# A graph-network stack on one Trainium2 core: one score slot in four joined into a single tile

## The chip, the cores and the metric

The kernel runs on one core of one Trainium2 chip. The metric is the device time of one launch in microseconds (us). The engines are TensorE (PE), VectorE (DVE), ScalarE (ACT) and GpSimd (POOL); SyncE (SP) issues most of the DMAs.

## The reference

Input x is 64 graphs of 256 nodes with 128 features, and one 256 x 256 matrix adj is shared by all. Four layers follow each other, each of the form x = x + L(relu(layernorm(x))). Layer 0 is a gated recurrence of five steps, layer 1 a Chebyshev filter, layer 2 a graph convolution with normalised rows. Layer 3 is pairwise attention, and most of the time is spent in it:

```python
s1 = jnp.einsum('bkf,ef->bke', x, W1)        # W = adj, W1, W2 its two halves
s2 = jnp.einsum('bkf,ef->bke', x, W2)
pre = s1[:, :, None, :] + s2[:, None, :, :] + b_lin
h = jnp.where(pre >= 0, pre, ALPHA * pre)     # ALPHA = 0.2
e = jnp.einsum('bije,e->bij', h, a) + bias
attn = jax.nn.softmax(e, axis=2)
out = jax.nn.sigmoid(jnp.einsum('bij,bjf->bif', attn, x))
```

For each graph, a score is needed for each pair (i, j) of 256 nodes; it is a sum over 256 features e of a leaky relu, weighted with a[e].

## The kernel before, in words

Two graphs make a pair; there are 32 pairs. The part of the score that is linear in s1 and s2 goes its own way (the row `lin`). What is left of the leaky relu is max(0, pre) with weight 0.8 a[e], and max(0, s1 + s2) is, up to terms that depend on one index or vanish in the softmax, -min(s1, -s2). So the work is a minimum per (graph, i, j, e), and then a weighted sum over e.

The 256 features are two **halves** of 128, one feature per partition: half 0 uses s1a and s2a, half 1 uses s1b and s2n. A **slot** is four nodes i (32 apart) of both graphs of a pair: for one half that is a tile `rl` of 128 partitions x 2048 numbers (4 nodes, 2 graphs, 256 nodes j). A pair has 64 slots, in two blocks of 32 (`ic`), and the whole kernel 2048 slots, so 4096 half-tiles. Three engines make them (`work_on_tile`, L723):

- VectorE makes half 0 in one instruction (L738), min(s1a, s2a), with s2a read in the PSUM bank that TensorE wrote it to (`s2v`, one bank for each parity of the pair).
- ScalarE makes either half with eight activations of 256 numbers (L751), relu(s1 - s2-type operand). For half 1 it reads `s2p`, a copy in a PSUM bank of its own (L745); for half 0 it reads `s2c`, a copy in SBUF that it makes once in a pair (L590).
- GpSimd makes half 1 with eight instructions of 256 numbers (L758), min(s2n, s1b) from SBUF and then max with the most negative number, which changes nothing.

TensorE sums each tile over the features with four matmuls (`score`, L783; L796) into one of two PSUM banks. Their weights are `win` or `win_n`, zero but for one column, which holds 0.8 a[e] or its negative; the window of 32 columns selects the row that the slot's node gets. After 64 tiles a block is full, and its `tail` (L635) makes the softmax and the output.

For each pair `front` (L392) computes the first three layers and the operands of the fourth; its last steps, from L584, write s2a, s2c, the row `lin`, s2n, s1b and s1a. `front` and `tail` are generators that yield before each step the engine and the time from which it can run.

The order of all instructions is fixed when the program is written. A planner (L846 to L876) keeps a clock for each engine, adds to it the cost written beside each step (`ran`, L101), and always lets the engine whose clock is earliest choose. Tails go ahead of fronts, and fronts ahead of tiles. `half` (L710) says which half an engine takes: VectorE half 0, GpSimd half 1, ScalarE half 1 unless half 0 is two slots or more behind (`LAG`). `MOST` bounds how many unscored tiles an engine may hold, and 13 tiles are shared by all. TensorE scores the tile that is ready earliest by that clock. `in_order` (L128) then binds each engine to the order found; the waits between engines come from who writes and reads which tile.

Of the kernel before, what the change touches and what calls it, by code (L numbers as in the profile page):

```python
# [8 lines left out]
F32 = mybir.dt.float32  # L9
# [8 lines left out]
LN_EPS = 1e-5  # L18
NORM_EPS = 1e-12
ALPHA = 0.2  # L20
LEAST = -3.4028234663852886e38
PE, DVE, ACT, POOL = ENGINES = (mybir.EngineType.PE, mybir.EngineType.DVE, mybir.EngineType.Activation, mybir.EngineType.Pool)
SLOTS = 64


@with_exitstack
def kernel(
# [168 lines left out]
    u5t = const.tile([P, P], F32, name="u5t")  # L196
    gate_b = const.tile([P, 3], F32, name="gate_b")
    bz, br, bh = gate_b[:, 0:1], gate_b[:, 1:2], gate_b[:, 2:3]
    th = const.tile([P, 3, D], F32, name="th")
    win = const.tile([P, NE, 63], F32, name="win")  # L200
    win_n = const.tile([P, NE, 63], F32, name="win_n")
    w2n = const.tile([P, N], F32, name="w2n")
    g2 = const.tile([P, P], F32, name="g2")
    SET_UP = set()

    def first_constants():
# [43 lines left out]
    def other_constants():  # L250

        yield DVE, 0.0, 0, lambda: "first" in SET_UP
        for c in range(NC):
            nc.vector.tensor_copy(adj_ti[:, c, :], adj_t[:, c, :])
            nc.vector.tensor_add(adj_ti[:, c, c * P:(c + 1) * P], adj_t[:, c, c * P:(c + 1) * P], ident)
        t = ran(DVE, 0.8)

        for c in range(NC):
            yield PE, t, 1
            b = take()  # L260
            for k in range(NC):
# [11 lines left out]
        nc.vector.memset(win, 0.0)  # L273
        nc.vector.memset(win_n, 0.0)
        nc.vector.tensor_scalar(w2n, adj_t[:, 1, :], -1.0, None, op0=OP.mult)
        ran(DVE, 0.6)
        yield DVE, clock[DVE]
        a_rep = work.tile([P, NE, P], F32, name="a_rep", tag="short", bufs=12)
        nc.vector.memset(a_rep, 1.0)
        for k in range(NE):  # L280
            nc.vector.tensor_scalar(win[:, k, 31:32], acol[:, k:k + 1], 1.0 - ALPHA, None, op0=OP.mult)
            nc.vector.tensor_scalar(win_n[:, k, 31:32], acol[:, k:k + 1], ALPHA - 1.0, None, op0=OP.mult)
            nc.vector.tensor_scalar(a_rep[:, k, :], a_rep[:, k, :], acol[:, k:k + 1], None, op0=OP.mult)
        t = ran(DVE, 1.2)

        yield PE, t, 1
# [3 lines left out]
        t = ran(PE, 0.8, t, b[1])  # L290
        yield DVE, t
        nc.vector.tensor_scalar(g2, b[0][:, 0:P], ALPHA, None, op0=OP.mult)
        t = ran(DVE, 0.25, t)
        spare.append([b[0], t])
        SET_UP.add("all")
# [51 lines left out]
    def tok(name, **kw):  # L347
        return work.tile([P, NB, NC, D], F32, name=name, **kw)
# [43 lines left out]
    def front(p):  # L392
# [101 lines left out]
                t_h = ran(ACT, COPY, t)  # L494
                spare.append([b[0], t_h])
        yield DVE, t
        x1 = tok("x1")
# [34 lines left out]
        x2 = tok("x2")  # L532
# [55 lines left out]
        yield ACT, t_s2a  # L588
        s2c = feat("s2c")
        nc.scalar.copy(s2c, by_feature(s2a))  # L590
        t_s2c = t_s2a = ran(ACT, COPY, t_s2a)
        yield PE, t_hT, 1
        b = take()
        for g in range(4):
            nc.tensor.matmul(b[0][g * 32:(g + 1) * 32, 0:P], g2[:, 0:32], flat(hT)[:, g * P:(g + 1) * P],  # L595
                             start=True, stop=True, skip_group_check=True)
        t = ran(PE, 0.22, t_hT, b[1])
        yield ACT, t
# [12 lines left out]
        t = ran(PE, PROJECT, t_hT, b[1])  # L611
        yield ACT, t
        s2n, t_2 = copied("s2n", b, t)
        yield PE, t_hT, 1
        b = take()
        project(b[0], adj_t[:, 0, P:2 * P], hT)
        t = ran(PE, PROJECT, t_hT, b[1])
        yield ACT, t
        s1b = feat("s1b")
        nc.scalar.activation(s1b, by_feature(b[0]), AF.Identity, bias=blin[:, 1:2], scale=1.0)  # L620
        t_b = ran(ACT, BIASED, t)
        spare.append([b[0], t_b])
        yield PE, t_hT, 1
        b = take()
        project(b[0], adj_t[:, 0, 0:P], hT)
        t = ran(PE, PROJECT, t_hT, b[1])
        yield ACT, t
        s1a = feat("s1a")
        nc.scalar.activation(s1a, by_feature(b[0]), AF.Identity, bias=blin[:, 0:1], scale=1.0)  # L629
        t_n = ran(ACT, BIASED, t)  # L630
        spare.append([b[0], t_n])
        READY[p] = dict(x3=x3, h3=h3, hT=hT, s1=(s1a, s1b), s2a=by_feature(s2a), s2c=s2c, s2n=s2n, lin=lin, t_lin=t_lin,
                        since=(max(t_n, t_s2a, t_s2c), max(t_b, t_2)))

    def tail(p, ic, pe, since, x3, h3):  # L635

# [56 lines left out]

    NSLOT = NPAIR * SLOTS
    tiles = [[relu_pool.tile([P, 4, NB, N], F32, name=f"rl{k}", bufs=1), 0.0] for k in range(13)]
    MOST = {DVE: 8, ACT: 3, POOL: 2}
    held = dict.fromkeys(MOST, 0)
    following = [0, 0]
    begun = {}
    made = []  # L700
    left = {}
    t_pe = {}
    LAG = 2
    t_s2v = [0.0, 0.0]
    TAILED = set()

    def where(n):
        return n // SLOTS, n % SLOTS // 32, n % 32

    def half(e):  # L710

        return 0 if e == DVE or e == ACT and following[0] <= following[1] - LAG else 1

    def tile_ready(e):

        if e in begun:
            return 0.0
        n = following[half(e)]
        if n >= NSLOT or n // SLOTS not in READY or held[e] == MOST[e] or not tiles:
            return None  # L720
        return max(READY[n // SLOTS]["since"][half(e)], min(t[1] for t in tiles))

    def work_on_tile(e):  # L723
        if e not in begun:
            k = half(e)
            tiles.sort(key=lambda t: t[1])
            begun[e] = [following[k], k, *tiles.pop(0), 0]
            following[k] += 1
# [5 lines left out]
        since = max(ops["since"][k], free)  # L734
        if e == DVE:
            whole = [P, 4, NB, N]
            rows = ops["s1"][0][:, :, i0:i0 + 97:32].rearrange("p b g -> p g b").unsqueeze(3)
            nc.vector.tensor_tensor(t, rows.to_broadcast(whole), ops["s2a"].unsqueeze(1).to_broadcast(whole), op=OP.min)  # L738
            done = ran(DVE, 2.2, since)
            t_s2v[p % 2] = done  # L740
            parts = 1
        elif e == ACT:
            if k and "s2p" not in ops:
                ops["s2p"] = s2p
                nc.scalar.copy(s2p, ops["s2n"])  # L745
                ran(ACT, COPY, since)
            parts = 2
            for g in (2 * part, 2 * part + 1):
                for b in range(NB):
                    i = i0 + g * 32  # L750
                    nc.scalar.activation(t[:, g, b, :], (s2p if k else ops["s2c"])[:, b, :], AF.Relu,  # L751
                                         bias=ops["s1"][k][:, b, i:i + 1], scale=-1.0)
            done = ran(ACT, 1.43 if k else 1.6, since)
        else:
            parts = 4
            for b in range(NB):
                i = i0 + part * 32
                nc.gpsimd.tensor_scalar(t[:, part, b, :], ops["s2n"][:, b, :], ops["s1"][1][:, b, i:i + 1], LEAST,  # L758
                                        op0=OP.min, op1=OP.max)
            done = ran(POOL, 0.9, since)  # L760
        begun[e][4] += 1
        if part + 1 == parts:
            del begun[e]
            made.append((done, n, k, t, e))

    def score_ready():

# [15 lines left out]
    def score(tile_):  # L783
# [5 lines left out]
        if first:  # L789
            left[block] = 64  # L790
        made.remove(tile_)
        left[block] -= 1

        w = win if e == ACT else win_n
        for g in range(4):
            nc.tensor.matmul(pe[g * 32:(g + 1) * 32, :], w[:, k, 31 - r:63 - r], flat(t[:, g]),  # L796
                             start=first, stop=(left[block] == 0), skip_group_check=True)
# [3 lines left out]
        scored[0] += 1  # L801
        if left[block] == 0:
            begin((p, ic), tail(p, ic, pe, free, READY[p]["x3"], READY[p]["h3"]))

# [103 lines left out]
```

## Time and profile before

| | |
|---|---|
| median of three runs | 5241.63 us (5241.58 to 5242.08) |
| profiled execution, its time | 5241.64 us |
| profiled execution, its span | 5239.9 us |
| TensorE clock granted, mean | 0.998 |
| GpSimd waiting for a tile that TensorE frees (L758) | 994.9 us, 384 times |
| GpSimd waiting for ScalarE in the recurrence (L474) | 347.6 us, 93 times |
| ScalarE waiting for a tile that TensorE frees (L751) | 137.9 us, 203 times |
| first tile begun | 120 us after the start |

A group of the profile is read so: line, engine, operation, output <- inputs, shapes, count; then busy time in all and the mean ns of one, and then the idle time of the engine before such instructions and what ended it. Neighbours on one engine overlap a little, so busy time divided by count is less than the mean of one, and is the one that adds up. A matmul of float32 leaves two records; a half-tile is eight of L796.

### The profile page before, as it was taken

What the parts mean: (1) busy time and instruction counts of PE and PEld (TensorE: products, weight loads), DVE (VectorE), ACT (ScalarE), POOL (GpSimd) and SP (SyncE); (2) the same over time, 40 slices, a digit from 0 to 9 for tenths busy, and PEclk for the clock granted to TensorE, in tenths of its full rate; (3) what the DMA queues carried; (4) which work ended last, traced back from release to release, by engine and by line L of the source; (5) the groups of instructions that cost most, each with busy time, mean ns of one, the idle gap of its engine ahead of it and who ended that gap; (6) DMA issues with size and microseconds to landing.
All of it is one profiled execution on the core that took longest, in us unless ns stands there. A gap on an engine that the chain in (4) does not pass through costs nothing.

```text
span 5239.9 us, 138951 instructions
## 1 busy us (share of the span) xinstructions
PE 5197.2 (99%) x56085; PEld 1856.9 (35%) x56085; DVE 5140.0 (98%) x4180; ACT 4563.7 (87%) x11785; POOL 3635.0 (69%) x7606
## 2 busy tenths in 40 slices
PE   7999999999999999999999999999999999999999
PEld 3333333333333333333333333333333333333333
DVE  3999999999999999999999999999999999999999
ACT  4888888888888888888888888888888888889899
POOL 2776766666766767667677676776666767767698
PEclk9999999999999999999999999999999999999999
DMA  0000000000000000000000000000000000000000
GB/s 20 7 8 5 8 8 5 8 5 8 8 5 8 5 8 8 5 8 7 6 8 6 8 8 5 8 8 5 8 5 8 8 5 8 6 7 6 5 6 4
DMA packets 60343, 37.48 MB, mean 7 GB/s; under 512 B 4528, under 2 KB 59696, under 8 KB 59696
## 3 DMA queue, kind: packets, MB, share of 16 engines
q1 hardware_dynamic: 58976, 28.59, 2.3%
q8 instruction: 438, 7.18, 0.6%
q14 instruction: 209, 1.71, 0.1%
q10 hardware_dynamic: 720, 0.00, 0.0%
HBM read 18.09 MB, written 10.49 MB: 5 GB/s over the span
## 4 chain that ended last, share of the span: by engine, by line
PE 92%; ACT 5%; DVE 2%; issue 0%; POOL 0%; DMA 0%; ACTq 0%; POOLq 0%
PE bank L796 61%; PE bank L306 27%; ACT rl L751 5%; PE bank L334 2%; DVE rl L738 2%; PE bank L327 1%; POOL rl L758 0%; PE bank L595 0%; DVE hT L481 0%; DVE stats L366 0%; ACT h L493 0%; DMA xin<-in_x_dram 0%; DVE bank L477 0%; DVE x L569 0%; POOL mv L301 0%
## 5 line engine op out<-in xcount | busy, mean ns | idle before, releaser
L738 DVE TENSOR_TENSOR rl<-s1a,bank 128x2048 f32<-128x2048 f32 x2028 | 4505.3, 2277 | 10.4 <-ACT s1a L629 10.1
L751 ACT ACTIVATE rl<-bank,s1b 128x256 f32<-128x256 f32 x9608 | 3691.7, 605 | 139.0 <-PE bank L796 137.9
L758 POOL TENSOR_SCALAR rl<-s2n,s1b 128x256 f32<-128x256 f32 x6776 | 3057.5, 475 | 1025.1 <-PE bank L796 994.9
L796 PE MATMUL bank<-rl,win_n 128*32 128x512 f32 x23000 | 2764.7, 593 | 6.2 <-DVE rl L738 6.0
L796 PE MATMUL bank<-rl,win 128*32 128x512 f32 x9768 | 1282.5, 593 | 0.0
L796 PEld LDWEIGHTS bank<-rl,win_n 128*32 128x32 f32 x23000 | 735.1, 110 | 1543.1 <-issue 1297.6
L796 PEld LDWEIGHTS bank<-rl,win 128*32 128x32 f32 x9768 | 307.0, 110 | 656.3 <-issue 620.7
L474 POOL TENSOR_TENSOR d<-d,hT 128x512 f32<-128x512 f32 x155 | 199.2, 1285 | 347.6 <-ACT d L470 347.6
L306 PE MATMUL bank<-mT,wts 128*32 128x512 f32 x2560 | 332.4, 592 | 0.0
L306 PE MATMUL bank<-adj_t,h 128*32 128x256 f32 x5120 | 309.5, 383 | 3.1 <-ACT h L493 3.1
L306 PEld LDWEIGHTS bank<-adj_t,h 128*32 128x32 f32 x5120 | 166.3, 111 | 164.2 <-issue 52.5
L383 ACT COPY mT<-bank 128x512 f32<-128x512 f32 x160 | 101.0, 631 | 99.4 <-PE bank L306 59.7
L377 ACT ACTIVATE h<-x,mv 128x128 f32<-128x128 f32 x384 | 172.0, 635 | 5.5 <-POOL mv L373 5.5
L657 ACT ACTIVATE sc<-sc,nmx 128x256 f32<-128x256 f32 x128 | 59.5, 523 | 132.5 <-DVE nmx L653 132.5
L306 PE MATMUL bank<-hT,wts 128*32 128x512 f32 x1280 | 167.1, 593 | 0.0
L306 PE MATMUL bank<-mT,w 128*32 128x512 f32 x1280 | 166.7, 592 | 0.0
L306 PE MATMUL bank<-rh,u5t 128*32 128x512 f32 x1280 | 166.6, 592 | 0.0
L493 ACT COPY h<-bank 128x512 f32<-128x512 f32 x128 | 92.1, 720 | 77.1 <-PE bank L334 76.8
L458 ACT ACTIVATE bank<-bank,gate_b 128x512 f32<-128x512 f32 x160 | 117.6, 735 | 44.2 <-PE bank L306 44.2
L306 PEld LDWEIGHTS bank<-mT,wts 128*32 128x32 f32 x2560 | 82.6, 110 | 192.1 <-issue 150.5
L435 ACT ACTIVATE bank<-bank,gate_b 128x512 f32<-128x512 f32 x160 | 118.8, 742 | 30.0 <-ACT rl L751 20.9
L301 POOL TENSOR_TENSOR mv<-mv,minus_half 128x4 f32<-128x4 f32 x128 | 133.0, 1039 | 10.7
(118 smaller groups left out, 3046.4 us busy)
## 6 DMA issues: line engine op xcount, KB each, us to landing
xin<-in_x_dram SPq DMA_DIRECT2D x64, 128.0 KB, 2.2
lin<-row SPq DMA_DIRECT2D x32, 256.0 KB, 7.7
out_dram<-o SPq DMA_DIRECT2D x64, 128.0 KB, 1.8
row<-quarter SPq DMA_DIRECT2D x32, 64.0 KB, 1.5
w_raw<-in_L_gnn_w_w_dram SPq DMA_DIRECT2D x3, 128.0 KB, 2.8
th_raw<-in_L_gnn_Theta_dram SPq DMA_DIRECT2D x1, 320.0 KB, 3.8
adj_n<-in_adj_dram SPq DMA_DIRECT2D x1, 256.0 KB, 3.4
w_raw<-in_L_gnn_u_w_dram SPq DMA_DIRECT2D x2, 64.0 KB, 3.0
```

Source lines behind the costliest of these rows:

```text
L301: nc.gpsimd.tensor_tensor(t, t, minus_half, op=OP.pow)
L306: nc.tensor.matmul(o[g:g + 32], w[:, g:g + 32], t, start=start, stop=stop, skip_group_check=True)
L334: nc.tensor.transpose(pt[:, b, c, :], ht[:, b, c * P:(c + 1) * P], ident)
L377: nc.scalar.activation(h[:, k, :], s[:, k, :], AF.Relu, bias=mv[:, k, 0:1], scale=mv[:, k, 1:2])
L383: nc.scalar.copy(c, by_feature(bank[0]))
L435: nc.scalar.activation(r[0], pr[0], AF.Tanh, bias=br, scale=0.5)
L458: nc.scalar.activation(pr[0], pr[0], AF.Tanh, bias=bz, scale=0.5)
L474: nc.gpsimd.tensor_sub(d, d, hT)
L738: nc.vector.tensor_tensor(t, rows.to_broadcast(whole), ops["s2a"].unsqueeze(1).to_broadcast(whole), op=OP.min)
L751: nc.scalar.activation(t[:, g, b, :], (s2p if k else ops["s2c"])[:, b, :], AF.Relu, bias=ops["s1"][k][:, b, i:i + 1], scale=-1.0)
L758: nc.gpsimd.tensor_scalar(t[:, part, b, :], ops["s2n"][:, b, :], ops["s1"][1][:, b, i:i + 1], LEAST, op0=OP.min, op1=OP.max)
L796: nc.tensor.matmul(pe[g * 32:(g + 1) * 32, :], w[:, k, 31 - r:63 - r], flat(t[:, g]), start=first, stop=(left[block] == 0), skip_group_che ...
```

## The change

Of every four slots one is **joined**. In a joined slot GpSimd makes half 1 as before, and VectorE then adds its minimum of half 0 into the same tile: eight `scalar_tensor_tensor` of 256 numbers, (s2a min s1a) + tile. TensorE sums this one tile in place of two. The other slots (`ALONE`) are made in two halves as before.

For one sum to serve both halves, the weights of the two halves on one partition may differ in sign only. The size 0.8 |a[e]| is therefore multiplied into the operands: `w1` and `w2n` are built in the set-up from adj_n scaled by `size` and transposed, and the bias becomes `blin_s`. `win` then holds only signs, and `win_n` the negative sign of half 0. Where the two signs on a partition differ (`rho` = -1), GpSimd's half must be negated: it reads `s2z` = rho x s2n, and clamps between two per-partition numbers, `s1h` and `s1l`, computed for each pair on VectorE from s1b with `never`.

Besides: `s2c` is gone, and ScalarE's half 0 reads s2a in the bank `s2v`, as VectorE does; its planned cost is 1.43 for either half. GpSimd may hold 4 tiles (before 2). It takes the next joined slot if that is at most `AHEAD_OF` = 4 slots past the next half 1 that stands alone, else that half 1. VectorE takes a finished partner tile before anything else, under a like condition. x1 and x2 share a tag of three buffers, th lies in th_raw, and win_n and g2 are smaller.

```diff
+SHARE = (1, 4)
+AHEAD_OF = 4
...
-        s2c = feat("s2c")
-        nc.scalar.copy(s2c, by_feature(s2a))
-        t_s2c = t_s2a = ran(ACT, COPY, t_s2a)
...
+        s2z = feat("s2z")
+        nc.gpsimd.tensor_scalar(s2z, s2n, rho, 1.0, op0=OP.mult, op1=OP.mult)
+        t_z = ran(POOL, 0.65, t_2)
...
-        nc.scalar.activation(s1b, by_feature(b[0]), AF.Identity, bias=blin[:, 1:2], scale=1.0)
+        nc.scalar.activation(s1b, by_feature(b[0]), AF.Identity, bias=blin_s[:, 1:2], scale=1.0)
...
+        s1h, s1l = feat("s1h"), feat("s1l")
+        nc.vector.tensor_scalar(s1h, s1b, never, None, op0=OP.max)
+        nc.vector.tensor_scalar(s1l, s1b, -1.0, never, op0=OP.mult, op1=OP.min)
+        t_z = max(t_z, ran(DVE, 0.8, t_b))
...
-    MOST = {DVE: 8, ACT: 3, POOL: 2}
+    MOST = {DVE: 8, ACT: 3, POOL: 4}
...
+    def part_of(e):
+
+        if e == DVE:
+            return 0
+        if e == ACT:
+            return 0 if following[0] <= following[1] - LAG else 1
+        return 2 if slot(2) <= slot(1) + AHEAD_OF else 1
...
-        if e == DVE:
+        if e == DVE and k == 2:
+            since = max(ops["since"][0], free)
+            parts = 2
+            for g in (2 * part, 2 * part + 1):
+                for b in range(NB):
+                    i = i0 + g * 32
+                    nc.vector.scalar_tensor_tensor(t[:, g, b, :], ops["s2a"][:, b, :], ops["s1"][0][:, b, i:i + 1], t[:, g, b, :],
+                                                   op0=OP.min, op1=OP.add)
+            done = ran(DVE, 1.55, since)
...
-                    nc.scalar.activation(t[:, g, b, :], (s2p if k else ops["s2c"])[:, b, :], AF.Relu,
+                    nc.scalar.activation(t[:, g, b, :], (s2p if k else ops["s2a"])[:, b, :], AF.Relu,
                                          bias=ops["s1"][k][:, b, i:i + 1], scale=-1.0)
-            done = ran(ACT, 1.43 if k else 1.6, since)
+            done = ran(ACT, 1.43, since)
...
-                nc.gpsimd.tensor_scalar(t[:, part, b, :], ops["s2n"][:, b, :], ops["s1"][1][:, b, i:i + 1], LEAST,
+                nc.gpsimd.tensor_scalar(t[:, part, b, :], ops["s2z"][:, b, :], ops["s1h"][:, b, i:i + 1], ops["s1l"][:, b, i:i + 1],
                                         op0=OP.min, op1=OP.max)
...
-            made.append((done, n, k, t, e))
+            if e == POOL and k == 2:
+                partners.append((done, n, t))
+            else:
+                made.append((done, n, k, t, e))
...
-        left[block] -= 1
-
-        w = win if e == ACT else win_n
+        left[block] -= 2 if k == 2 else 1
+
+        w = win[:, k] if e == ACT else win_n
```

More of the change, by code (lines that the diff above doesn't have):

```diff
@@ L20 @@
 ALPHA = 0.2
-LEAST = -3.4028234663852886e38
+MOST_NEGATIVE = -3.4028234663852886e38
 PE, DVE, ACT, POOL = ENGINES = (mybir.EngineType.PE, mybir.EngineType.DVE, mybir.EngineType.Activation, mybir.EngineType.Pool)
 SLOTS = 64
+SHARE = (1, 4)
+AHEAD_OF = 4
 @with_exitstack
@@ L198 @@
     bz, br, bh = gate_b[:, 0:1], gate_b[:, 1:2], gate_b[:, 2:3]
-    th = const.tile([P, 3, D], F32, name="th")
+    th = th_raw[:, 0:3, :]
     win = const.tile([P, NE, 63], F32, name="win")
-    win_n = const.tile([P, NE, 63], F32, name="win_n")
+    win_n = const.tile([P, 63], F32, name="win_n")
+    w1 = const.tile([P, N], F32, name="w1")
     w2n = const.tile([P, N], F32, name="w2n")
-    g2 = const.tile([P, P], F32, name="g2")
+    g2 = const.tile([P, 32], F32, name="g2")
+    signs = const.tile([P, NE + 2], F32, name="signs")
+    rho, never = signs[:, NE:NE + 1], signs[:, NE + 1:NE + 2]
+    blin_s = const.tile([P, NE], F32, name="blin_s")
     SET_UP = set()
@@ L272, in other_constants @@
         yield DVE, clock[DVE]
[L273 to L277, printed above, removed]
         a_rep = work.tile([P, NE, P], F32, name="a_rep", tag="short", bufs=12)
@@ L280, in other_constants @@
         for k in range(NE):
-            nc.vector.tensor_scalar(win[:, k, 31:32], acol[:, k:k + 1], 1.0 - ALPHA, None, op0=OP.mult)
-            nc.vector.tensor_scalar(win_n[:, k, 31:32], acol[:, k:k + 1], ALPHA - 1.0, None, op0=OP.mult)
             nc.vector.tensor_scalar(a_rep[:, k, :], a_rep[:, k, :], acol[:, k:k + 1], None, op0=OP.mult)
-        t = ran(DVE, 1.2)
-        yield PE, t, 1
+        t_a = ran(DVE, 0.9)
+        yield DVE, clock[DVE]
+        nc.vector.memset(win, 0.0)
+        nc.vector.memset(win_n, 0.0)
+        nc.vector.tensor_scalar(signs[:, 0:NE], acol, 0.0, None, op0=OP.is_ge)
+        nc.vector.tensor_scalar(signs[:, 0:NE], signs[:, 0:NE], 2.0, -1.0, op0=OP.mult, op1=OP.add)
+        nc.vector.tensor_mul(rho, signs[:, 0:1], signs[:, 1:2])
+        nc.vector.tensor_scalar(never, rho, MOST_NEGATIVE, None, op0=OP.mult)
+        size = work.tile([P, NE], F32, name="size")
+        nc.vector.tensor_mul(size, acol, signs[:, 0:NE])
+        nc.vector.tensor_scalar(size, size, 1.0 - ALPHA, None, op0=OP.mult)
+        nc.vector.tensor_mul(blin_s, blin, size)
+        adj_s = work.tile([P, NE, N], F32, name="adj_s", tag="short", bufs=12)
+        for k in range(NE):
+            nc.vector.tensor_copy(win[:, k, 31:32], signs[:, k:k + 1])
+            nc.vector.tensor_scalar(adj_s[:, k, :], adj_n[:, k, :], size[:, k:k + 1], None, op0=OP.mult)
+        nc.vector.tensor_scalar(win_n[:, 31:32], signs[:, 0:1], -1.0, None, op0=OP.mult)
+        t = ran(DVE, 2.4)
+        for c in range(NC):
+            yield PE, t, 1
+            b = take()
+            for k in range(NE):
+                nc.tensor.transpose(b[0][:, k * P:(k + 1) * P], adj_s[:, k, c * P:(c + 1) * P], ident)
+            t = ran(PE, 0.4, t, b[1])
+            yield DVE, t
+            if c:
+                nc.vector.tensor_scalar(w2n, b[0][:, 0:N], -1.0, None, op0=OP.mult)
+            else:
+                nc.vector.tensor_copy(w1, b[0][:, 0:N])
+            t = ran(DVE, 0.35, t)
+            spare.append([b[0], t])
+        yield PE, t_a, 1
         b = take()
@@ L289, in other_constants @@
             nc.tensor.matmul(b[0][:, 0:P], adj_n[:, k, P:2 * P], a_rep[:, k, :], start=(k == 0), stop=(k == NE - 1))
-        t = ran(PE, 0.8, t, b[1])
+        t = ran(PE, 0.8, t_a, b[1])
         yield DVE, t
-        nc.vector.tensor_scalar(g2, b[0][:, 0:P], ALPHA, None, op0=OP.mult)
+        nc.vector.tensor_scalar(g2, b[0][:, 0:32], ALPHA, None, op0=OP.mult)
         t = ran(DVE, 0.25, t)
@@ L496, in front @@
         yield DVE, t
-        x1 = tok("x1")
+        x1 = tok("x1", tag="x12", bufs=3)
         nc.vector.tensor_add(x1, x0, by_token(b[0]))
@@ L531, in front @@
         yield DVE, clock[DVE]
-        x2 = tok("x2")
+        x2 = tok("x2", tag="x12", bufs=3)
         nc.vector.scalar_tensor_tensor(x2, by_token(po[0]), 0.0, x1, op0=OP.max, op1=OP.add)
@@ L587, in front @@
         t_s2a = ran(PE, PROJECT, t_hT, t_s2v[p % 2])
-        yield ACT, t_s2a
-        s2c = feat("s2c")
-        nc.scalar.copy(s2c, by_feature(s2a))
-        t_s2c = t_s2a = ran(ACT, COPY, t_s2a)
         yield PE, t_hT, 1
@@ L594, in front @@
         for g in range(4):
-            nc.tensor.matmul(b[0][g * 32:(g + 1) * 32, 0:P], g2[:, 0:32], flat(hT)[:, g * P:(g + 1) * P],
+            nc.tensor.matmul(b[0][g * 32:(g + 1) * 32, 0:P], g2, flat(hT)[:, g * P:(g + 1) * P],
                              start=True, stop=True, skip_group_check=True)
@@ L613, in front @@
         s2n, t_2 = copied("s2n", b, t)
+        yield POOL, t_2
+        s2z = feat("s2z")
+        nc.gpsimd.tensor_scalar(s2z, s2n, rho, 1.0, op0=OP.mult, op1=OP.mult)
+        t_z = ran(POOL, 0.65, t_2)
         yield PE, t_hT, 1
         b = take()
-        project(b[0], adj_t[:, 0, P:2 * P], hT)
+        project(b[0], w1[:, P:2 * P], hT)
         t = ran(PE, PROJECT, t_hT, b[1])
@@ L619, in front @@
         s1b = feat("s1b")
-        nc.scalar.activation(s1b, by_feature(b[0]), AF.Identity, bias=blin[:, 1:2], scale=1.0)
+        nc.scalar.activation(s1b, by_feature(b[0]), AF.Identity, bias=blin_s[:, 1:2], scale=1.0)
         t_b = ran(ACT, BIASED, t)
         spare.append([b[0], t_b])
+        yield DVE, t_b
+        s1h, s1l = feat("s1h"), feat("s1l")
+        nc.vector.tensor_scalar(s1h, s1b, never, None, op0=OP.max)
+        nc.vector.tensor_scalar(s1l, s1b, -1.0, never, op0=OP.mult, op1=OP.min)
+        t_z = max(t_z, ran(DVE, 0.8, t_b))
         yield PE, t_hT, 1
         b = take()
-        project(b[0], adj_t[:, 0, 0:P], hT)
+        project(b[0], w1[:, 0:P], hT)
         t = ran(PE, PROJECT, t_hT, b[1])
@@ L628, in front @@
         s1a = feat("s1a")
-        nc.scalar.activation(s1a, by_feature(b[0]), AF.Identity, bias=blin[:, 0:1], scale=1.0)
+        nc.scalar.activation(s1a, by_feature(b[0]), AF.Identity, bias=blin_s[:, 0:1], scale=1.0)
         t_n = ran(ACT, BIASED, t)
         spare.append([b[0], t_n])
-        READY[p] = dict(x3=x3, h3=h3, hT=hT, s1=(s1a, s1b), s2a=by_feature(s2a), s2c=s2c, s2n=s2n, lin=lin, t_lin=t_lin,
-                        since=(max(t_n, t_s2a, t_s2c), max(t_b, t_2)))
+        READY[p] = dict(x3=x3, h3=h3, hT=hT, s1=(s1a, s1b), s2a=by_feature(s2a), s2n=s2n, s2z=s2z, s1h=s1h, s1l=s1l,
+                        lin=lin, t_lin=t_lin, since=(max(t_n, t_s2a), max(t_b, t_2), t_z))
     def tail(p, ic, pe, since, x3, h3):
@@ L695 @@
     tiles = [[relu_pool.tile([P, 4, NB, N], F32, name=f"rl{k}", bufs=1), 0.0] for k in range(13)]
-    MOST = {DVE: 8, ACT: 3, POOL: 2}
+    MOST = {DVE: 8, ACT: 3, POOL: 4}
     held = dict.fromkeys(MOST, 0)
-    following = [0, 0]
     begun = {}
     made = []
+    partners = []
     left = {}
@@ L705, with slot @@
     TAILED = set()
+    ALONE, JOINED = [], []
+    for n in range(NSLOT):
+        (JOINED if (n + 1) * SHARE[0] // SHARE[1] > n * SHARE[0] // SHARE[1] else ALONE).append(n)
+    following = [0, 0, 0]
     def where(n):
         return n // SLOTS, n % SLOTS // 32, n % 32
-    def half(e):
-        return 0 if e == DVE or e == ACT and following[0] <= following[1] - LAG else 1
+    def slot(k):
+        of = JOINED if k == 2 else ALONE
+        return of[following[k]] if following[k] < len(of) else NSLOT
+    def part_of(e):
[4 more added lines that the diff above has]
+        return 2 if slot(2) <= slot(1) + AHEAD_OF else 1
     def tile_ready(e):
@@ L717, in tile_ready @@
             return 0.0
-        n = following[half(e)]
+        if e == DVE and partners and min(partners)[1] <= slot(0) + AHEAD_OF:
+            return min(partners)[0]
+        k = part_of(e)
+        n = slot(k)
         if n >= NSLOT or n // SLOTS not in READY or held[e] == MOST[e] or not tiles:
             return None
-        return max(READY[n // SLOTS]["since"][half(e)], min(t[1] for t in tiles))
+        since = READY[n // SLOTS]["since"]
+        return max(since[2] if e == POOL else since[k], min(t[1] for t in tiles))
     def work_on_tile(e):
         if e not in begun:
[L725 to L728, printed above, removed]
+            if e == DVE and partners and min(partners)[1] <= slot(0) + AHEAD_OF:
+                since, n, t = partners.pop(partners.index(min(partners)))
+                held[POOL] -= 1
+                begun[e] = [n, 2, t, since, 0]
+            else:
+                k = part_of(e)
+                tiles.sort(key=lambda t: t[1])
+                begun[e] = [slot(k), k, *tiles.pop(0), 0]
+                following[k] += 1
             held[e] += 1
@@ L733, in work_on_tile @@
         i0 = ic * P + r
-        since = max(ops["since"][k], free)
-        if e == DVE:
+        if e == DVE and k == 2:
[7 more added lines that the diff above has]
+            done = ran(DVE, 1.55, since)
+            t_s2v[p % 2] = max(t_s2v[p % 2], done)
+        elif e == DVE:
+            since = max(ops["since"][k], free)
             whole = [P, 4, NB, N]
@@ L739, in work_on_tile @@
             done = ran(DVE, 2.2, since)
-            t_s2v[p % 2] = done
+            t_s2v[p % 2] = max(t_s2v[p % 2], done)
             parts = 1
         elif e == ACT:
+            since = max(ops["since"][k], free)
             if k and "s2p" not in ops:
@@ L750, in work_on_tile @@
                     i = i0 + g * 32
-                    nc.scalar.activation(t[:, g, b, :], (s2p if k else ops["s2c"])[:, b, :], AF.Relu,
+                    nc.scalar.activation(t[:, g, b, :], (s2p if k else ops["s2a"])[:, b, :], AF.Relu,
                                          bias=ops["s1"][k][:, b, i:i + 1], scale=-1.0)
-            done = ran(ACT, 1.43 if k else 1.6, since)
+            done = ran(ACT, 1.43, since)
+            if k == 0:
+                t_s2v[p % 2] = max(t_s2v[p % 2], done)
         else:
+            since = max(ops["since"][2], free)
             parts = 4
@@ L763, in work_on_tile @@
             del begun[e]
-            made.append((done, n, k, t, e))
+            if e == POOL and k == 2:
+                partners.append((done, n, t))
+            else:
+                made.append((done, n, k, t, e))
     def score_ready():
@@ L791, in score @@
         made.remove(tile_)
-        left[block] -= 1
-        w = win if e == ACT else win_n
+        left[block] -= 2 if k == 2 else 1
+        w = win[:, k] if e == ACT else win_n
         for g in range(4):
-            nc.tensor.matmul(pe[g * 32:(g + 1) * 32, :], w[:, k, 31 - r:63 - r], flat(t[:, g]),
+            nc.tensor.matmul(pe[g * 32:(g + 1) * 32, :], w[:, 31 - r:63 - r], flat(t[:, g]),
                              start=first, stop=(left[block] == 0), skip_group_check=True)
@@ L800, in score @@
         held[e] -= 1
-        scored[0] += 1
+        scored[0] += 2 if k == 2 else 1
         if left[block] == 0:
```

## The prediction

> **What bounds the kernel now.** I read the page first: the busy shares, then the chain that ended last.
>
> ```profile
> PE 5197.2 (99%) x56085; PEld 1856.9 (35%) x56085; DVE 5140.0 (98%) x4180; ACT 4563.7 (87%) x11785; POOL 3635.0 (69%) x7606
> ...
> PE 92%; ACT 5%; DVE 2%; issue 0%; POOL 0%; DMA 0%; ACTq 0%; POOLq 0%
> ```
>
> The chain is 92% PE, so TensorE sets the end; VectorE is as full, but the chain hardly visits it. The table of windows shows the same balance in the middle:
>
> ```profile
> 2000.00:3000.00 1000.00, 999.16 (x10803) 355.78 (x10796) 998.56 (x797) 877.44 (x2270) 693.63 (x1447) 1.00 0.03 7
> ```
>
> Then the groups by form, which price the tiles:
>
> ```profile
> L738 DVE TENSOR_TENSOR rl<-s1a,bank 128x2048 f32<-128x2048 f32 x2028 | 4505.3, 2277 | 10.4 <-ACT s1a L629 10.1 <-issue 0.3
> L751 ACT ACTIVATE rl<-bank,s1b 128x256 f32<-128x256 f32 x9608 | 3691.7, 605 | 139.0 <-PE bank L796 137.9
> L758 POOL TENSOR_SCALAR rl<-s2n,s1b 128x256 f32<-128x256 f32 x6776 | 3057.5, 475 | 1025.1 <-PE bank L796 994.9 <-ACT s1b L620 8.3 <-ACT rl L751 6.5
> ...
> L751 ACT ACTIVATE rl<-s2c,s1a 128x256 f32<-128x256 f32 x160 | 79.9, 1146 | 0.0
> ```
>
> There are 2048 slots of two half-tiles. VectorE makes 2028 first halves at 4505.3/2028 = 2.22 us each (busy time over count: neighbours overlap, so the mean of one is longer). ScalarE makes 9608/8 = 1201 second halves at 3.07 us and 160/8 = 20 first halves; GpSimd 847 at 3.61 us, with 995 us of waiting for a tile that PE frees. The last row matters most: ScalarE's first halves come from s2c, a copy in SBUF, and nearly none exist. VectorE reads the same numbers in the PSUM bank itself. So today no bank is read by both.
>
> PE's price comes from the chain in order of time, VectorE's from its timeline:
>
> ```profile
> 2513.68 10.30 PE bank L796 x96
> ```
> ```profile
> 2510.34 0.68 DVE L439 SCALAR_TENSOR_TENSOR rh<-bank,hT 128x512 f32<-128x512 f32 x1
> 2510.94 11.07 DVE L738 TENSOR_TENSOR rl<-s1a,bank 128x2048 f32<-128x2048 f32 x5
> ```
> ```profile
> 5033.00 1.12 DVE L569 SCALAR_TENSOR_TENSOR x<-bank,rn,x 128x128 f32<-128x128 f32 x4
> 5034.03 2.28 DVE L738 TENSOR_TENSOR rl<-s1a,bank 128x2048 f32<-128x2048 f32 x1
> ```
>
> 96 records are 12 tiles of 8, so 0.858 us a tile. L439 occupies VectorE from start to next start for 0.60 us at 512 elements, L569 (with a per-partition scalar) 1.03/4 = 0.258 us at 128.
>
> **What the Trainium skill says.** "PSUM — Partial Sum Buffer", section "PSUM bank collisions raise a hardware error": two engines on one bank and 32-partition quadrant at once collide, ScalarE reads against VectorE reads included, without arbitration; the compiler back end therefore adds a dependency between any two such instructions, "reads and writes alike". The trace of before can't confirm it: the only rows that could share the bank read s2c instead. "VectorE: DVE Perf Modes", section "The perf-mode tier table": a tensor_tensor with a PSUM operand runs at 1x. It agrees: 2048 elements in 2.20 us. "GPSIMD Engine Reference", section "Key points": GpSimd contends with VectorE instructions that have two SBUF inputs. L738 has one SBUF and one PSUM input, and L758 stays at 463 to 506 ns; the new instruction has the same pair, so I add nothing.
>
> **The change, part by part.** The sum is made against the profiled execution: 5241.64 us, span 5239.9, equal to the median 5241.63.
>
> *PE.* 512 of 2048 slots are joined: 512 tiles fewer at 0.858 us = -439 us. All of it lies on the path. The two set-up transposes lie in the first 120 us, where PE waits anyway; at most 2 us. PE's floor: 5241.6 - 439 = 4802 us.
>
> *VectorE.* A joined half costs 8 scalar_tensor_tensor of 256 elements with a per-partition scalar. L738's slope is 2.20 us/2048 = 1.07 ns per element. L569 at 128 elements is 0.137 of that plus a fixed 0.12; so at 256 elements 0.27 + 0.12 = 0.39 us, and 3.13 us for the eight. Bounds: 0.33 (with the fixed part of L439, 0.60 - 512 x 0.00107 = 0.05, which has no such scalar) and 0.48 (with the whole record of L569, 0.343, as if nothing overlapped); 512 x 8 x 0.09 = 370 us at the upper one. 512 x 3.13 = 1603 us. s1h and s1l add 64 instructions of 512 elements at up to 0.60 (L439's) = 38 us. Other work is 5140.0 - 4505.3 = 635. Idle at start and end is 95 (80 + 12, rounded up). The some fifteen small set-up operations hide in the start; 3 us if they don't.
>
> *ScalarE.* s2c's 32 copies go (25 us). First halves are now read from VectorE's bank. How many? The planner gives ScalarE a first half when VectorE is two behind. If its plan comes to about 4850 us (the PE floor and 1%), VectorE has room for (4850 - 95 - 673 - 1603)/2.22 = 1116 of the 1536 alone, and ScalarE takes n = 420.
>
> *GpSimd.* 512 x 3.61 us for the joined halves go first, the rest for second halves. Its second pointer scalar: between 0 and the 0.06 us that L569 shows over L439; taken as 0, since GpSimd has 31% free. s2z is 32 instructions below 0.95 us (twice L758), 30 us at most, hidden in the front's slack.
>
> *The new waits.* VectorE waits for GpSimd's half; the planner queues it only when its clock says done, and that clock (3.6 us) is L758's. Behind it all of VectorE's queue would stand, and PE behind that; I count 0, at most 0.5 us x 512 = 256 if the second scalar costs its bound. The other wait isn't in the planner's clock: **if reads of one bank exclude each other, every batch of four ScalarE activations on a first half must stand between two VectorE instructions.** Behind VectorE's head stand its tiles, the partners and the front's steps, thus everybody. The length of a batch:
>
> ```profile
> 2554.12 0.91 ACT L657 ACTIVATE sc<-sc,nmx 128x256 f32<-128x256 f32 x2 [1.80 <-DVE nmx L653]
> 2554.94 1.54 ACT L751 ACTIVATE rl<-bank,s1b 128x256 f32<-128x256 f32 x4
> ```
>
> A batch lasts 1.54 to 1.58 us. Handover to ScalarE: L653 ended at 2554.09, L657 began at 2554.12, 0.03; back, L470's end to L474's start on GpSimd is 0.07. VectorE also loses the 0.08 by which the record of L738 overhangs its 2.20. One gap is 0.03 + 1.56 + 0.07 + 0.08 = 1.74 us; two batches in a row 3.2. With a 1.43 us batch in the plan, VectorE's next 2.2 us instruction comes between the two in 0.65 of cases, so a tile costs VectorE 0.65 x 3.48 + 0.35 x 3.2 = 3.38 us. Some is filled with its steps that don't touch the bank (673 of 4850 us, 14%): I take 10% off, leaving 3.05. Bounds: 0 to all 673 us hidden.
>
> Sum on VectorE, n = 420: 95 + 673 + 1603 + 1116 x 2.2215 + 420 x 3.05 = 2371 + 2479 + 1281 = **6131 us**. As a function of n it is 5783 + 0.83n: a first half handed to ScalarE costs VectorE more than making it. So n matters little (300: 6032; 500: 6198). I say 6130; own range 5600 (nearly all other VectorE work inside the gaps) to 6600 (further stalls because a fixed order with two-way waits also passes on ScalarE's delays).
>
> The rest costs nothing on this path: x1 and x2 share three buffers (the third reuse waits for the x2 of the pair before, on VectorE itself, long done); th lies in th_raw; win_n and g2 shrink; w1, blin_s are set up once; no DMA is added or moved, SP's queue keeps its order.
>
> **Rivals.** *A, reads exclude each other*, 6130 us. For: the skill's page, and the diff, which takes away the copy and with it the only separation of the two readers. Against: the planner's clock has no such wait, and no trace here shows one.
>
> *B, the reads run side by side.* Then supply decides. With VectorE (T - 2371)/2.22, ScalarE (T - 95 - 767)/3.05, GpSimd (T - 95 - 608 - 1848)/3.61 equal to 3072 halves together, T = 4860 if all three never wait; with 2% of idle 4950. This is **faster**, by 5.5%. It decides if ScalarE's batches begin while VectorE reads the bank. For: PE loses 439 us for certain, and ScalarE and GpSimd have 13% and 31% idle. Against: the three idle shares vanish together.
>
> *C, exclusion, but mostly beside other work.* The bank itself is taken 1603 + 2479 + 420 x 2.86 = 5283 us, with the first 120 us about 5400. For: 673 us of VectorE and most of ScalarE don't need the bank. Against: the order is fixed, so overlap needs luck.
>
> *The change doesn't do what it says*: joined slots could be few if GpSimd lagged. The list of slots is fixed in the text at 512, so this has no weight.
>
> **How the numbers follow.** A 0.78, B 0.14, C 0.07, and 0.01 that gains and waits cancel. About 0.2% is what a measurement of this kernel can tell from no change. Faster 0.14, same 0.01, slower 0.85. The range takes C and A with their bounds, 5250 to 6600, and leaves out B and a little of A's upper tail.
>
> **What would show it.** Right: VectorE idle of over 1000 us before rl, released by ScalarE's activations, and ScalarE idle before first halves, released by VectorE; some 3300 activations on bank and s1a; PE near 78% busy; the chain divided between DVE and ACT; the new instruction near 0.39 us. Wrong: those activations beside VectorE's instructions on the same bank without a wait (then B), or few of them at all (then about 5800 or less).

## The result, and the profile after

The changed kernel takes 6100.69 us in the median of four runs (6098.29 to 6101.25), the kernel before 5241.85 beside it: 1.164 times as long, with a 95% interval of 1.162 to 1.166. The forecast was 6130 us. The profiled execution has a span of 6099.1 us.

First the busy shares and the chain on the page of the changed kernel, to be held against the first fence of the prediction.

```profile
PE 5222.9 (86%) x51993; PEld 1790.7 (29%) x51993; DVE 4849.6 (80%) x7435; ACT 4821.7 (79%) x12465; POOL 5531.7 (91%) x10142
...
DVE 10%; ACT 5%; PE 2%; POOL 1%; issue 1%; ACTq 0%; DVEq 0%; POOLq 0%
```

PE is no longer full, and neither are VectorE (98% before) and ScalarE (87% before). No engine is full; GpSimd comes nearest, at 91% where it was at 69%. The chain's shares add up to only 19%, so this view can't say what sets the end; the waits have to. Next, the groups by form that answer to those of before (here L804 is the old L738, L818 the old L751, L828 the old L758, and L796 is the new instruction).

```profile
L828 POOL TENSOR_SCALAR rl<-s2z,s1h,s1l 128x256 f32<-128x256 f32 x9280 | 4940.7, 552 | 13.0 <-DVE s1l L655 13.0
L818 ACT ACTIVATE rl<-bank,s1b 128x256 f32<-128x256 f32 x7104 | 2751.3, 577 | 2.0 <-PE bank L869 0.5 <-ACT bank L812 0.4
...
L804 DVE TENSOR_TENSOR rl<-s1a,bank 128x2048 f32<-128x2048 f32 x1114 | 2515.0, 2281 | 680.1 <-ACT rl L818 665.4 <-PE bank L869 10.1 <-ACT s1a L663 2.8
L796 DVE SCALAR_TENSOR_TENSOR rl<-bank,s1a,rl 128x256 f32<-128x256 f32 x4096 | 1670.2, 475 | 459.4 <-ACT rl L818 391.0 <-POOL rl L828 56.6 <-ACT c1T L412 2.9
...
L818 ACT ACTIVATE rl<-bank,s1a 128x256 f32<-128x256 f32 x3376 | 1322.2, 497 | 1031.0 <-DVE rl L796 579.4 <-DVE rl L804 430.4 <-PE bank L869 9.2
```

The last columns tell the story. VectorE stood idle 665 + 391 = 1056 us before its tiles until an activation of ScalarE ended, and ScalarE 579 + 430 = 1010 us before its first halves (rl<-bank,s1a) until an instruction of VectorE ended. ScalarE's second halves (rl<-bank,s1b), on a bank of their own, wait for next to nothing (2.0 us). The two engines pass no data to each other there: each makes its own tile. What they share is that both read s2a in the bank `s2v`. The timelines of VectorE and of ScalarE for the same few microseconds (start, duration, idle before) show it happening.

```profile
3004.47 0.68 DVE L468 SCALAR_TENSOR_TENSOR rh<-bank,hT 128x512 f32<-128x512 f32 x1
3006.19 2.29 DVE L804 TENSOR_TENSOR rl<-s1a,bank 128x2048 f32<-128x2048 f32 x1 [1.03 <-ACT rl L818]
3010.11 4.49 DVE L804 TENSOR_TENSOR rl<-s1a,bank 128x2048 f32<-128x2048 f32 x2 [1.64 <-ACT rl L818]
```
```profile
3004.59 1.57 ACT L818 ACTIVATE rl<-bank,s1a 128x256 f32<-128x256 f32 x4 [1.27 <-DVE rl L796]
3008.51 1.57 ACT L818 ACTIVATE rl<-bank,s1a 128x256 f32<-128x256 f32 x4 [2.35 <-DVE rl L804]
```

ScalarE's batch (four activations, half a tile) ends at 3006.16, VectorE starts at 3006.19 and ends at 3008.48, ScalarE starts at 3008.51 and ends at 3010.08, VectorE starts at 3010.11. They take turns, and while one reads, the other is idle. At 3004.47 VectorE had a step that doesn't touch the bank (L468), and in these few microseconds only that stretch overlaps.

The whole trace says the same. Of the 1322 us of ScalarE's first halves, 18 us lie beside a VectorE instruction that works on a tile, in 13 places, each within 4 us of ScalarE's turn to a new pair (its copy at L812), when the two engines can be at different pairs and so at different banks of `s2v`. In e1 below, where ScalarE reads a copy, it is 1038 us of 1358.

### The profile page after: what moved, and what is told of

Read it like the earlier page. It is cut to its first block, busy times and chain, and to the rows that moved or that the text cites. A ratio compares the mean times of both kernels' runs of the same rounds, so it can differ in the third digit from the quotient of the medians.

```text
span 6099.1 us, 136803 instructions
## 1 busy us (share of the span) xinstructions
PE 5222.9 (86%) x51993; PEld 1790.7 (29%) x51993; DVE 4849.6 (80%) x7435; ACT 4821.7 (79%) x12465; POOL 5531.7 (91%) x10142
## 5 line engine op out<-in xcount | busy, mean ns | idle before, releaser
L828 POOL TENSOR_SCALAR rl<-s2z,s1h,s1l 128x256 f32<-128x256 f32 x9280 | 4940.7, 552 | 13.0 <-DVE s1l L655 13.0
L804 DVE TENSOR_TENSOR rl<-s1a,bank 128x2048 f32<-128x2048 f32 x1114 | 2515.0, 2281 | 680.1 <-ACT rl L818 665.4
L869 PE MATMUL bank<-rl,win_n 128*32 128x512 f32 x18192 | 2557.4, 615 | 303.6 <-DVE rl L804 247.9
L818 ACT ACTIVATE rl<-bank,s1b 128x256 f32<-128x256 f32 x7104 | 2751.3, 577 | 2.0 <-PE bank L869 0.5
L818 ACT ACTIVATE rl<-bank,s1a 128x256 f32<-128x256 f32 x3376 | 1322.2, 497 | 1031.0 <-DVE rl L796 579.4
L796 DVE SCALAR_TENSOR_TENSOR rl<-bank,s1a,rl 128x256 f32<-128x256 f32 x4096 | 1670.2, 475 | 459.4 <-ACT rl L818 391.0
L869 PE MATMUL bank<-rl,win 128*32 128x512 f32 x10480 | 1499.9, 613 | 0.0
L869 PEld LDWEIGHTS bank<-rl,win_n 128*32 128x32 f32 x18192 | 609.0, 112 | 1765.8 <-issue 817.4
L363 PE MATMUL bank<-ident,hT 128*128 128x128 f32 x640 | 121.7, 321 | 271.0 <-DVE hT L510 256.0
L503 POOL TENSOR_TENSOR d<-d,hT 128x512 f32<-128x512 f32 x155 | 198.6, 1281 | 156.8 <-ACT d L499 155.6
L683 POOL TENSOR_TENSOR sc<-sc,lin 128x512 f32<-128x512 f32 x63 | 80.3, 1275 | 141.8 <-DVE sc L673 136.0
```

What stands on the lines that cost most here:

```text
L363: nc.tensor.transpose(pt[:, b, c, :], ht[:, b, c * P:(c + 1) * P], ident)
L503: nc.gpsimd.tensor_sub(d, d, hT)
L683: nc.gpsimd.tensor_add(sc, sc, ops["lin"])
L796: nc.vector.scalar_tensor_tensor(t[:, g, b, :], ops["s2a"][:, b, :], ops["s1"][0][:, b, i:i + 1], t[:, g, b, :], op0=OP.min, op1=OP.add)
L818: nc.scalar.activation(t[:, g, b, :], (s2p if k else ops["s2a"])[:, b, :], AF.Relu, bias=ops["s1"][k][:, b, i:i + 1], scale=-1.0)
L828: nc.gpsimd.tensor_scalar(t[:, part, b, :], ops["s2z"][:, b, :], ops["s1h"][:, b, i:i + 1], ops["s1l"][:, b, i:i + 1], op0=OP.min, op1=OP.max)
```

## The experiments

Each starts from the changed kernel, and the diffs show only the lines that matter. The first four separate two suspects that the profile after names: the shared bank, and GpSimd's instruction, which grew from 475 to 552 ns.

**e1: ScalarE gets a copy of s2a in SBUF.** It is made at the pair's first such tile; hT3 (another operand) gets one buffer less to make room, and the planned cost of a ScalarE batch on a first half is again 1.6.

```diff
+            if k == 0 and "s2c" not in ops:
+                ops["s2c"] = s2c
+                nc.scalar.copy(s2c, ops["s2a"])
...
-                    nc.scalar.activation(t[:, g, b, :], (s2p if k else ops["s2a"])[:, b, :], AF.Relu,
+                    nc.scalar.activation(t[:, g, b, :], (s2p if k else s2c)[:, b, :], AF.Relu,
```

> ScalarE reads its first halves from an SBUF copy of s2a, made once per pair, in place of VectorE's bank; all else is as in the changed kernel. Theory (reads of one bank exclude each other, and that makes the loss): the waits of VectorE's tiles for ScalarE's and the other way round, 1056 and 1010 us in the changed kernel, fall under 100 us each. The time then stops at GpSimd, whose 5532 us of work in the changed kernel (552 ns an instruction, where the planner counts 450) plus 100 us at start and end and some waits give 5650 to 5850 us. Rival 1 (GpSimd's slower instruction alone is the loss): the time stays at 6050 to 6150 us though those waits go. Rival 2 (only the bank stood in the way, GpSimd keeps up): 4950 us.

Measured: 5752.24 us, 1.099 of the kernel before (1.096 to 1.102). The groups and, from the list of waits, what VectorE waited for longest:

```profile
L831 POOL TENSOR_SCALAR rl<-s2z,s1h,s1l 128x256 f32<-128x256 f32 x9352 | 5014.0, 571 | 8.0 <-DVE s1l L655 8.0
...
L805 DVE TENSOR_TENSOR rl<-s1a,bank 128x2048 f32<-128x2048 f32 x1138 | 2555.7, 2277 | 10.5 <-ACT s2c L817 7.0 <-ACT s1a L663 2.9 <-PE bank L872 0.5
L797 DVE SCALAR_TENSOR_TENSOR rl<-bank,s1a,rl 128x256 f32<-128x256 f32 x4096 | 1747.4, 476 | 150.1 <-POOL rl L831 91.6 <-ACT s2c L817 11.8 <-issue 0.2
...
L823 ACT ACTIVATE rl<-s2c,s1a 128x256 f32<-128x256 f32 x3184 | 1357.5, 575 | 1.3
```
```profile
DVE bank L506 <- POOL d L503: 349.7, 129, 6.5
DVE rl L797 <- POOL rl L831: 91.6, 87, 2.7
```

The mutual waits are gone: ScalarE's 1031 us of idle before its first halves fell to 1.3, and VectorE's 1056 us before its tiles to the 7.0 + 11.8 us in which ScalarE makes the copy, the one read of that bank that it still has. ScalarE still makes 3184/8 = 398 first halves (422 in the changed kernel), so the waits did not go for want of them. The shared bank was their cause. But the kernel is still 10% slower than before, and now the limit is GpSimd. Two lines of the page show it:

```profile
PE 5312.6 (92%) x51993; PEld 1852.3 (32%) x51993; DVE 4992.0 (86%) x7459; ACT 4823.9 (83%) x12233; POOL 5598.4 (97%) x10214
...
POOL 75%; PE 11%; DVE 7%; ACT 3%; issue 3%; POOLq 0%; DMA 0%; ACTq 0%; DVEq 0%
```

GpSimd is 97% busy and holds 75% of the chain; VectorE waits 350 us for the recurrence's step on GpSimd (L503), while that step itself waits only 54 us for its input from ScalarE: it stands in GpSimd's queue behind tiles.

**e3: GpSimd's second clamp is the constant again.** The bank stays shared. This kernel leaves out GpSimd's minimum on the partitions where the two signs differ, so it can only price the scalar.

```diff
-                nc.gpsimd.tensor_scalar(t[:, part, b, :], ops["s2z"][:, b, :], ops["s1h"][:, b, i:i + 1], ops["s1l"][:, b, i:i + 1],
+                nc.gpsimd.tensor_scalar(t[:, part, b, :], ops["s2z"][:, b, :], ops["s1h"][:, b, i:i + 1], MOST_NEGATIVE,
```

> GpSimd's second clamp is again a constant, the most negative number, in place of the per-partition s1l; this leaves out the negated half where the signs differ. The sharing of the bank stays. It prices the second per-partition scalar: theory, 475 ns an instruction as in the kernel before, against 552 in the changed kernel. If the second scalar isn't what makes it slow (contention with VectorE or the s2z operand instead), it stays near 550. On the time: exclusion theory 6000 to 6110 us, since GpSimd's slack isn't on the path; rival (GpSimd is the limit): 5300 us or less.

Measured: 6094.22 us, 1.163 (1.161 to 1.165). GpSimd's group, and one of VectorE's:

```profile
L828 POOL TENSOR_SCALAR rl<-s2z,s1h 128x256 f32<-128x256 f32 x9280 | 4184.2, 475 | 91.3 <-PE bank L869 50.0 <-DVE s1h L654 15.1 <-ACT rl L818 3.3
...
L804 DVE TENSOR_TENSOR rl<-s1a,bank 128x2048 f32<-128x2048 f32 x1114 | 2515.3, 2282 | 682.1 <-ACT rl L818 669.1 <-PE bank L869 6.8 <-ACT s1a L663 2.8
```

The instruction is back at 475 ns, from the same operand s2z and beside the same VectorE work. The second per-partition scalar costs (4940.7 - 4184.2)/9280 = 82 ns. And 756 us less work on GpSimd brings 6 us, so little that the intervals of the two kernels overlap, and VectorE's waits for ScalarE stay (669 us). While the bank is shared, GpSimd's speed hardly matters.

**e4: both at once.** The copy of e1 and the constant of e3; the same part is left out here.

> Both at once: ScalarE reads its own SBUF copy for first halves, and GpSimd's second clamp is a constant (the negated half is left out). With neither the shared bank nor the slower GpSimd instruction, the prediction's rival B should appear: 4860 us if no engine waits, 4950 us with 2% of idle; 4900 to 5050 us. If it stays above 5241 us there is a third cost that neither theory has.

Measured: 5034.62 us, 0.961 (0.959 to 0.962). The page:

```profile
PE 4890.0 (97%) x51993; PEld 1795.2 (36%) x51993; DVE 4856.8 (97%) x7459; ACT 4786.0 (95%) x12233; POOL 4810.4 (96%) x10214
```

All four engines are 95 to 97% busy. No third cost of any size is left. The four kernels make a square:

| | GpSimd with two scalars | with one |
|---|---|---|
| bank shared | 6100.69 (the change) | 6094.22 (e3) |
| ScalarE reads a copy | 5752.24 (e1) | 5034.62 (e4) |

The second scalar costs 6 us in the upper row and 718 us in the lower, with the planner's costs as they are. Two limits lie one behind the other, and the farther one shows only when the nearer is gone.

**e2: ScalarE takes no first halves.** The bank has one reader without any copy.

```diff
-            return 0 if following[0] <= following[1] - LAG else 1
+            return 1
```

> ScalarE takes no first half any more; VectorE makes all 1536 that stand alone. Nobody but VectorE reads the bank of s2a. Theory (exclusion): the prediction's line 5783 + 0.83n at n = 0, with the joined instruction at its measured 0.408 us: 95 + 673 + 1670 + 1536 x 2.2215 = 5850 us, so faster than the changed kernel's 6100 though VectorE gets 937 us more work; VectorE over 97% busy. Rival (GpSimd is the limit): not below 6050 us, or above it, with VectorE waiting for GpSimd.

Measured: 5816.71 us, 1.110 (1.108 to 1.111). The busy shares, and VectorE's tiles:

```profile
PE 5344.8 (92%) x51993; PEld 1910.7 (33%) x51993; DVE 5697.9 (98%) x7857; ACT 5394.2 (93%) x14193; POOL 2850.7 (49%) x5038
...
L804 DVE TENSOR_TENSOR rl<-s1a,bank 128x2048 f32<-128x2048 f32 x1536 | 3440.6, 2276 | 0.0
...
L796 DVE SCALAR_TENSOR_TENSOR rl<-bank,s1a,rl 128x256 f32<-128x256 f32 x4096 | 1656.7, 473 | 0.0
```

VectorE made 422 tiles more, 926 us of work, and the kernel became 284 us faster. VectorE's idle before these rows is 0.0, and it is 98% busy, so VectorE's own work sets the time, 33 us from the sum of 5850.

**e5: the copy, and a planner that knows GpSimd's cost.** `ran(POOL, 0.9, since)` becomes `ran(POOL, 1.08, since)`; the computation is whole. In the expectation below, "supply" is the time at which the half-tiles that the three engines can make add up to those that are needed.

> ScalarE's own copy of s2a as before in these runs, GpSimd's instruction whole (two per-partition scalars), and the planner told its true cost, 1.08 us for two in place of 0.9, so that it gives GpSimd fewer halves that stand alone. Theory (the 5752 us of the run with the copy alone were a plan that overloads GpSimd by a fifth): with 4.4 us a half on GpSimd the three engines' supply gives 5100 us without idle; the run with both costs gone lay 3.6% above its own such figure, so 5200 to 5300 us. Rival (GpSimd's slow instruction itself is the loss, whatever the plan): 5600 us or more.

Measured: 5229.08 us, 0.998 (0.997 to 0.998). GpSimd's group:

```profile
L831 POOL TENSOR_SCALAR rl<-s2z,s1h,s1l 128x256 f32<-128x256 f32 x8160 | 4373.4, 556 | 8.2 <-DVE s1l L655 6.8 <-PE bank L335 1.4
```

The time is inside the expected range, and the rival's 5600 us is far off. It is 523 us faster than e1 with the same kinds of instructions; GpSimd got 8160 of them in place of 9352. So of the 718 us between e1 and e4, 523 were an order planned for a faster GpSimd than there is. The other 194 us (5229.08 - 5034.62) are what the second scalar still costs with that one figure put right.

**e6, e7, e8: the second scalar only where it is needed, and fewer joined slots.** Halves that GpSimd makes for slots that stand alone need no negation; they read s2n and s1b as in the kernel before, with weights of their own sign (the lines that build these weights are not shown). e6 joins one slot in four, e7 one in six, e8 one in eight.

```diff
+                if k == 2:
+                    nc.gpsimd.tensor_scalar(t[:, part, b, :], ops["s2z"][:, b, :], ops["s1h"][:, b, i:i + 1], ops["s1l"][:, b, i:i + 1],
+                                            op0=OP.min, op1=OP.max)
+                else:
+                    nc.gpsimd.tensor_scalar(t[:, part, b, :], ops["s2n"][:, b, :], ops["s1"][1][:, b, i:i + 1], MOST_NEGATIVE,
+                                            op0=OP.min, op1=OP.max)
+            done = ran(POOL, 1.08 if k == 2 else 0.91, since)
```

> The same, but where GpSimd makes a half that stands alone it reads s2n and s1b and clamps with the constant, as in the kernel before, with weights of that half's own sign; only joined halves pay for the second scalar. Supply: 4992 us without idle, plus 3.6%: 5120 to 5220 us, below the kernel before.

> The same with one slot in six joined. PE's floor rises to 5242 - 341 x 0.858 = 4949 us, the supply's figure without idle falls to 4888 us: 5030 to 5100 us. If the balance of floor and supply decides, this is better than one in four; if joining itself pays, it is worse.

> The same with one slot in eight joined: PE's floor 5242 - 256 x 0.858 = 5022 us, supply 4835 us without idle, so PE is the limit again: 5040 to 5100 us, with PE 98% busy.

| run | joined | us | of the kernel before |
|---|---|---|---|
| e6 | 1 in 4 | 5148.61 | 0.983 (0.981 to 0.984) |
| e7 | 1 in 6 | 5006.94 | 0.955 (0.954 to 0.957) |
| e8 | 1 in 8 | 5060.97 | 0.965 (0.964 to 0.967) |

e7 is the fastest kernel here, 23 us below the range expected of it; e6 and e8 lie inside theirs. All three compute the whole result. The page of e7, then the chains of e6 and of e8:

```profile
PE 4937.4 (99%) x53361; PEld 1785.6 (36%) x53361; DVE 4863.6 (97%) x6342; ACT 4728.0 (94%) x12121; POOL 4799.5 (96%) x9694
...
PE 52%; DVE 13%; POOL 4%; ACT 3%; issue 1%; ACTq 0%; DVEq 0%; POOLq 0%
```
```profile
DVE 33%; PE 26%; POOL 24%; ACT 14%; issue 2%; DMA 0%; POOLq 0%; ACTq 0%; DVEq 0%
```
```profile
PE 75%; DVE 15%; ACT 5%; POOL 4%; issue 1%; DMA 0%; DVEq 0%; SPq 0%; ACTq 0%; POOLq 0%
```

In e7 PE is full and the other three nearly so. With fewer joined slots (e8) PE holds 75% of the chain and ScalarE has room (89% busy); with more (e6) no engine is over 97% busy and PE holds only 26% of the chain.

## Why the prediction was right, and where it wasn't

**The mechanism** (case A, given 0.78) is the one that happened. e1 shows it: take the second reader from the bank, and the waits on both sides vanish. The releasers in the trace are semaphore events (signals by which one engine lets another go on), and VectorE's queue shows 233 semaphore instructions at L796 against 20 in e1, so this is order written into the program. That agrees with the Trainium skill ("PSUM — Partial Sum Buffer", section "PSUM bank collisions raise a hardware error"), which says that the compiler back end adds a dependency between two engines' instructions on one bank, reads included. Which tool wrote the order here, and what the chip would do without it, no run shows.

**The number of shared tiles** was forecast as 420; it is 3376/8 = 422, and VectorE kept 1114, forecast 1116.

**VectorE's work.** Tiles alone 2515 us (2479 forecast: 2.258 us each instead of 2.22; 401 of them start after a gap, so the 0.08 us that a record overhangs is not hidden by the one before, an estimated 32 us in all), joined halves 1670 (1603: 0.408 us an instruction instead of 0.39; unrounded, the forecast's 0.27 + 0.12 is 0.395, which is 15 of the 67 us), the rest 4849.6 - 2515.0 - 1670.2 = 664 (673). In sum 95 us more than forecast.

**VectorE's idle time** was forecast as 95 at the ends and 1281 in gaps. It is 6099.1 - 4849.6 = 1250, of which 1056 us are the gaps. They are 626 gaps (401 at L804 and 225 at L796) of 1.69 us. The forecast had 1.74 for a single batch, with the 0.08 of overhang that the trace counts as work, and 3.2 for two in a row. It had 1.65 gaps a tile; 626/422 = 1.48 came. The missing gaps were filled: of the 1322 us of ScalarE's first halves, 253 ran beside VectorE's other steps, where the 10% taken off comes to 420 x (3.38 - 3.05) = 139. Of the rest, 57 us are waits for GpSimd's half (0 forecast, bound 256), and 137 stand against the 95 at the ends. In sum the idle time is 126 us less than forecast. The two errors leave 31 us: that the total came within 0.5% is in part luck.

**The line 5783 + 0.83n**, which said that a half handed to ScalarE costs VectorE more than making it, was tested by e2 at n = 0: 5817 us. The sign holds; the slope between the two kernels is (6100.69 - 5816.71)/422 = 0.67 us a tile instead of 0.83.

**The step that failed is GpSimd's.** It was "between 0 and the 0.06 us that L569 shows over L439; taken as 0, since GpSimd has 31% free". The scalar costs 0.082 us, over the bound, which had been read from VectorE and didn't carry over to another engine. And the 31% were those of the kernel before: with 6776 instructions GpSimd had 6776 x 0.451 + 578 = 3635 us of work, and with 9280 of the slower ones it has 5532. In case A this hides behind the bank (e3: 6 us). But it makes the time of **rival B** wrong: with reads side by side, 4950 us was forecast, and e1, the nearest run to that case, took 5752. The 0.14 given to a faster kernel rested on that forecast, and e1 is 10% slower than the kernel before. With the constant back (e4) rival B's reckoning holds to 1.7% of 5035, which is 3.6% above its figure without idle where 2% was assumed. **Rival C's** overlap came in part: the 253 us are somewhat over a third of VectorE's 664 us of other work.

**What would show it.** "PE near 78% busy" failed: it is 86%, though PE has 512 tiles less. PE's busy time for each record rose from 5197.2/56085 = 0.093 to 5222.9/51993 = 0.100 us, while the mean record of the scoring matmuls (`win_n`) rose from 593 to 615 ns and the granted clock fell from 0.998 to 0.962. No run separates a lower clock from matmuls that start alone. Either way, PE's busy share was no measure of its load here. "The chain divided between DVE and ACT" could not be read from a chain that covers 19%.

## What to carry to other kernels

Before an operand in PSUM gets a second reader, ask whether the two engines' reads are kept apart; here they took turns, each turn cost VectorE a batch and two handovers (1.69 us), and a copy made once per pair was far cheaper (e1: -348 us, e3 to e4: -1060). Price an added operand by a row of the same engine, and where an order is written out by a planner, correct the planner with it: the plan's error cost 523 us (e1 to e5). A saving on the full engine is worth only what the others can follow: a joined slot saves PE 0.858 us but costs VectorE 8 x 0.408 = 3.26 us where a half that stands alone costs 2.22, and VectorE was 98% busy before. That is 512 x 1.04 = 532 of the 575 us by which e2, without any shared bank, is longer than the kernel before. So tune the share: one in six gave 0.955 where one in four gave 0.983. Whether a planner that knows of the turns could keep the bank shared at a smaller loss, no run here tries.

## What the runs showed that was not expected

A second per-partition scalar on a GpSimd tensor_scalar of 256 numbers raises it from 475 to 552 ns (e3 and the changed kernel). It went up once more, to 571 ns in the mean and 565 in the median, in the profiled execution of e1, where GpSimd was 97% busy, but not in e5 (556) at 95%. That execution took 5785.25 us, 33 us more than the other three of e1, and 9352 x (0.536 - 0.532) us is about as much; so the others may not have had it. Its cause stays open. VectorE's instruction with the half in place held 472 to 476 ns a record in all of them.
